# TensorE's queue in traced order, woven from four chains, with score products of four heads side by side

## The chip, the cores and the metric

The kernel runs on one core of a Trainium2 chip. The metric is the device time of one execution in microseconds; a kernel's time is the median of its runs. In the text PE is TensorE's matmuls, PEld its weight loads, DVE VectorE, ACT ScalarE, POOL GpSimd and SP the queue that issues most DMAs. `L382` is line 382 of the kernel before, unless the text says that it is of the one after.

## The reference, cut to what matters

Eight sequences of 512 tokens with 128 channels pass two layers. Everything is float32.

```python
# layer 0
h  = layernorm(x) * (1 + ca) + sa
xn = ln1(h)
attn = softmax(mask(q k^T / sqrt(8))) v        # 16 heads of 8, causal, 512 x 512
xc = silu(conv4(xn @ in_x));  dt = softplus(...);  B, C from xc @ x_proj
for t:  s = exp(dt A) s + dt xc B;  y = C s    # 256 channels, 16 states, 512 steps
y  = (y + xc D) * silu(xn @ in_z)
h  = h + alpha (attn @ o_w) + (1 - alpha) (y @ ssm_out)
h  = h + gelu(ln2(h) @ f1) @ f2;   x = x + ga * h
hm = layernorm(x) * (1 + cb) + sb
x  = x + gb * (shared(hm) + sum over the 2 best of 8 experts of gate * expert(hm))
# layer 1: attention over the 8 sequences at one position (8 heads), then
xr, xk = mixes of x and x one token earlier
x  = x + gb * sigmoid(xr Wr) * (relu(xk Wk)^2 Wv)
```

An expert is `silu(hm @ We1) @ We2` with a hidden width of 512. The kernel computes all eight and the shared one for every token, and weights them.

## The kernel before, in words

Activations lie with channels on the partitions, one sequence ("batch" b) as a tile of 128 x 512. All batches' residuals stay in `xT` (L146). A scheduler puts the instructions of each engine in an order, from the order of tracing, the buffers and its own idea of times; every engine then works through its own queue in that order. Buffers of a pool with the same tag are used in turn, and a tile waits until the readers of the one before in its buffer are done.

Layer 0, for each batch b:
- `head` (L620) loads x, does two layer norms and then `ssm_inputs` (L496): convolution, gates, B and C, and dt. B and C go to memory and are read back to all partitions. `layernorm` (L206) is a chain: mean by a matmul (L209), subtraction on DVE (L211), square on ACT (L213), variance by eight small matmuls (L217), power -0.5 on POOL (L226), spreading by matmuls (L230), product on DVE (L237), scale on ACT (L240).
- `ssm_scan` (L572) does the recurrence: in 8 steps of two states for each of two channel halves, ACT makes `da` (L585), DVE makes `hs` (L589) and scans it twice (L593), POOL multiplies by C (L596), DVE and POOL add it up (L604, L605). `so` (L611) projects the result.
- `attention` (L344) works on four groups g of four heads, each head on 32 partitions. `maxima` (L361) makes q and k (L364, L370), then per pair of heads and query block `qi` two score products of 32 rows (L382), two mask products (L390) and the negative row maximum on DVE (L393). `values` (L401) transposes the maxima (L406), adds them to q (L411), and per pair and key block `kj` makes the transposed scores (L419), masks (L427), the exponential on ACT (L431) and two value products of 32 columns (L435). `projected` (L446) divides by the sums (L452, L460, L464, L471) and projects (L474).
- `tail` (L631) does ln2, the feed-forward part (L639, L643, L648), a layer norm and `routing` (L665), a row of small DVE operations. `experts` (L733) does nine experts: four first products (L745), SiLU on ACT (L749), four accumulating second products (L756), the weighting (L764) and the sum on POOL (L767). `dispatch` (L722) sends the gates to memory; L753 reads one expert's gates to all partitions.

Scores lie in the pool `psc` (two buffers of two banks), values in `pacc` (one bank), all other products in `pmm` (three buffers of one bank, one tag).

The order of tracing is made by `together` (L197), which takes a piece of each of its parts in turn, up to a `yield`. For each batch the parts are attention b; the scan of b, and after it the head of b+1; `finish` of b-1 (tail and experts); and from b = 3 twelve pieces of layer 1's attention of a pair of batches (`attention2`, L254):

```python
            together(
                attention(b, xn, h),
                chain(ssm_scan(b, h, *scanned), head(b + 1) if b + 1 < NB else ()),
                behind or (),
                islice(second, 12) if second else (),
            )
```

Layer 1 takes the last pair's attention, adds all attentions to `xT` (L812), and then treats batch after batch from L821: layer norm, two mixes (L828, L831), three products (L836, L840, L845), a transposition (L852) and the store.

Of the kernel before, what the change touches and what calls it, by code (L numbers as in the profile page):

```python
# [33 lines left out]
EPS = 1e-5  # L34

# [36 lines left out]
def kernel(  # L72
# [20 lines left out]
    pmm = ctx.enter_context(tc.tile_pool(name="pmm", bufs=3, space=PSUM))  # L93
    psc = ctx.enter_context(tc.tile_pool(name="psc", bufs=2, space=PSUM))
    pacc = ctx.enter_context(tc.tile_pool(name="pacc", bufs=1, space=PSUM))
    dram = ctx.enter_context(tc.tile_pool(name="dram", bufs=2, space=DRAM))
    io = ctx.enter_context(tc.tile_pool(name="io", bufs=2))
    lnp = ctx.enter_context(tc.tile_pool(name="lnp", bufs=2))
# [48 lines left out]


    mods = []
    with tc.tile_pool(name="modp", bufs=1) as modp:  # L150
# [3 lines left out]
        for l in range(2):  # L154
# [6 lines left out]
            ps = pmm.tile([P, 512], F32, tag="mm", name=f"modps{l}")  # L161
# [35 lines left out]
    def together(*parts):  # L197

        parts = [iter(p) for p in parts]
        while parts:  # L200
            parts = [p for p in parts if next(p, parts) is None]

    def mm_tile(name):
        return pmm.tile([P, 512], F32, tag="mm", name=name)

    def layernorm(dst, src, scale, bias, name):  # L206

        mps = mm_tile(f"{name}_m")
        nc.tensor.matmul(mps, lhsT=mean_w, rhs=src, start=True, stop=True)  # L209
        d = lnp.tile([P, T], F32, tag="ln_d", name=f"{name}_d")  # L210
        nc.vector.tensor_sub(d, src, mps)  # L211
        sq = lnp.tile([P, T], F32, tag="ln_s", name=f"{name}_s")
        nc.scalar.activation(sq, d, AF.Square)  # L213

        vps = mm_tile(f"{name}_v")
# [8 lines left out]
        sd = lnp.tile([P, NTT], F32, tag="ln_r", name=f"{name}_r")  # L224
        nc.vector.tensor_scalar(sd, vps[:, :NTT], EPS, None, ALU.add)
        nc.gpsimd.tensor_tensor(sd, sd, mhalf, ALU.pow)  # L226

        rps = mm_tile(f"{name}_rb")
# [11 lines left out]
        nc.scalar.activation(dst, d, AF.Identity, bias=bias, scale=scale)  # L240

# [12 lines left out]
    def attention2(sp, at):  # L254

        hT = at.tile([P, NB, 2, U], F32, tag="pr", name=f"hT{sp}")
        for k in range(2):
            b = 2 * sp + k
            layernorm(hT[:, :, k, :], xT[:, b, :], mod(1, 1, b), mod(1, 0, b), f"lnc{b}")
            yield  # L260
        qkv = at.tile([P, NB, 3, C], F32, tag="qkv", name=f"qkv{sp}", bufs=1)
        for i in range(NB):
            ps = mm_tile(f"qkv{sp}_{i}")
            nc.tensor.matmul(
                ps[:, : 3 * C],
                lhsT=hT[:, i, :, :].rearrange("p s u -> p (s u)"),
                rhs=cwb("qkv"),
                start=True,
                stop=True,
            )  # L270
            nc.vector.tensor_add(
                qkv[:, i, :, :].rearrange("p k c -> p (k c)"), ps[:, : 3 * C], crow("qkv_b")
            )
            if i % 2:
                yield

        sc = at.tile([P, NB, NB, H1], F32, tag="sc", name=f"sc{sp}", bufs=1)
        for i in range(NB):
            pr = at.tile([P, NB, C], F32, tag="pr", name=f"pr{sp}_{i}")
# [9 lines left out]
            yield  # L289
# [17 lines left out]
        for i in range(NB):  # L307
            pr = at.tile([P, NB, C], F32, tag="pr", name=f"pv{sp}_{i}")
# [9 lines left out]
            yield  # L318
# [3 lines left out]
    def load_x(b):  # L322
        xin = io.tile([P, NTT, C], F32, tag="xio", name=f"xin{b}")
        nc.sync.dma_start(out=xin, in_=x[b].rearrange("(j p) c -> p j c", p=P))
        ps = mm_tile(f"xT{b}")
# [4 lines left out]
    with ExitStack() as l0:  # L330
        act = l0.enter_context(tc.tile_pool(name="act", bufs=1))
# [12 lines left out]
        def attention(b, xn, h):  # L344
# [4 lines left out]
            for j in range(NTT):  # L349
                ps = mm_tile(f"v{b}_{j}")  # L350
                nc.tensor.matmul(
                    ps[:, : NH * HV],
                    lhsT=xn[:, j * P : (j + 1) * P],
                    rhs=cw("v"),
                    start=True,
                    stop=True,
                )
                nc.vector.tensor_add(va[:, j, : NH * HV], ps[:, : NH * HV], crow("v_b"))
            qTs, kTs, sums = {}, {}, {}

            def maxima(g):  # L361

                ps = mm_tile(f"q{b}_{g}")
# [5 lines left out]
                ps = mm_tile(f"k{b}_{g}")  # L369
# [5 lines left out]
                qTs[g], kTs[g] = qT, kT  # L375
                for pr in range(2):
                    for qi in range(NTT):
                        n = (qi + 1) * P
                        ps = psc.tile([P, 2, 512], F32, tag="sc", name=f"s{b}_{g}_{pr}_{qi}")
                        for j in range(2):  # L380
                            q4 = quadrant(2 * pr + j)
                            nc.tensor.matmul(  # L382
                                ps[:, j, :n],
                                lhsT=qT[q4, qi * P : n],
                                rhs=kT[q4, :n],
                                start=True,
                                stop=False,
                            )
                        for j in range(2):
                            nc.tensor.matmul(  # L390
                                ps[:, j, qi * P : n], lhsT=ident_b, rhs=mask_b, start=False, stop=True
                            )
                        nc.vector.tensor_reduce(  # L393
                            mpads[g % 2][:, qi, 2 * pr : 2 * pr + 2, HD : HD + 1],
                            ps[:, :, :n],
                            AX.X,
                            ALU.max,
                            negate=True,
                        )

            def values(g):  # L401

                qT, kT = qTs.pop(g), kTs.pop(g)
                ps = mm_tile(f"mT{b}_{g}")
# [6 lines left out]
                nc.vector.tensor_add(qT, qT, ps)  # L411
                av = pacc.tile([P, T], F32, tag="acc", name=f"av{b}_{g}")
                for pr in range(2):
                    for kj in range(NTT):
                        n = T - kj * P
                        ps = psc.tile([P, 2, 512], F32, tag="sc", name=f"e{b}_{g}_{pr}_{kj}")
                        for j in range(2):
                            q4 = quadrant(2 * pr + j)
                            nc.tensor.matmul(  # L419
                                ps[:, j, :n],  # L420
                                lhsT=kT[q4, kj * P : (kj + 1) * P],
                                rhs=qT[q4, kj * P :],
                                start=True,
                                stop=False,
                            )
                        for j in range(2):
                            nc.tensor.matmul(  # L427
                                ps[:, j, :P], lhsT=ident_b, rhs=maskT_b, start=False, stop=True
                            )
                        ex = wk.tile([P, 2, T], F32, tag="ex", name=f"ex{b}_{g}_{pr}_{kj}")  # L430
                        nc.scalar.activation(ex[:, :, :n], ps[:, :, :n], AF.Exp)  # L431
                        for j in range(2):
                            i = 2 * pr + j
                            c0 = (4 * g + i) * HV
                            nc.tensor.matmul(  # L435
# [50 lines left out]
            for g in range(NG):  # L486
                if g + 1 < NG:
                    maxima(g + 1)
                    yield
# [502 lines left out]
```

## Time and profile before

| | us |
|---|---|
| runs | 2850.2, 2853.29, 2853.92; median 2853.29 |
| profiled execution | 2842.39 |
| its span, first to last instruction | 2840.6 |
| mean granted PE clock | 0.756 of full |
| first score maximum / last, batch 0 | 66 / 203 |
| last score maximum, batch 7 | 2385 |
| first score maxima of batches 1 to 7 | 317, 628, 926, 1263, 1566, 1905, 2208 |
| last batch: attention and scan done / first SiLU of experts / experts done | 2462 / 2525 / 2591 |
| last layer's first layer norm | 2658 |

The page shows the busy time of each engine, then the span in 40 equal slices, where a digit is the busy share in tenths. PEclk is the granted PE clock in the same slices: a matmul lasts twice as long at 5. A busy PE can be a slow one, so PE's work is best compared as busy time multiplied by the clock. A query by stretches gives, for each stretch, the busy time of PE, PEld, DVE, ACT and POOL (in brackets the number of instructions), then the clock, the DMA share and GB/s. A timeline row gives start, duration, engine, line, tiles, shapes and how many instructions were merged; in brackets, idle time before it and what ended it. An f32 product is two matmul instructions.

### The profile page before, as it was taken

The numbers are of one execution on the slowest core, as the hardware profiler recorded it, in microseconds if no ns is written. First come the engines' busy times: TensorE is split into PE (matmuls) and PEld (weight loads), VectorE is DVE, ScalarE is ACT, GpSimd is POOL, SyncE is SP. The second block draws the span as 40 slices with busy tenths as digits, with TensorE's granted clock in tenths as the row PEclk, the third lists the DMA queues.
The fourth block names the chain that finished last, engine by engine and source line by source line (L and its number), as shares of the span: only waits on it lengthen the run. The fifth ranks groups of instructions, "written<-read, shape, count | busy, mean of one in ns | idle before, by whom it ended". The sixth has DMA issues, their size and how long they took to land. (4 is left out here: it accounts for less than half of the span.)

```text
span 2840.6 us, 22315 instructions
## 1 busy us (share of the span) xinstructions
PE 2224.3 (78%) x8408; PEld 984.8 (35%) x8408; DVE 1394.0 (49%) x1734; ACT 1054.5 (37%) x1409; POOL 996.5 (35%) x587
## 2 busy tenths in 40 slices
PE   5888689878887689878987689878887689986355
PEld 3333233433343333433343333333343333433222
DVE  2861684158513864358513964358513864312522
ACT  3221434353445234353445234353435234332111
POOL 2550353036303553246203553236202553303311
PEclk9556658976898669876797769876797759888555
DMA  3100111121012101121012101121012101111000
GB/s 108 60 30 4 63 57 38 37 79 67 27 37 83 59 23 34 34 79 67 27 38 81 58 24 36 30 79 67 27 34 75 60 26 38 49 52 37 4 11 15
DMA packets 58923, 131.60 MB, mean 46 GB/s; under 512 B 6552, under 2 KB 14880, under 8 KB 58688
## 3 DMA queue, kind: packets, MB, share of 16 engines
q1 hardware_dynamic: 58336, 127.83, 14.6%
q10 hardware_dynamic: 288, 1.93, 0.2%
q8 instruction: 66, 1.08, 0.2%
q0 software_dynamic: 192, 0.42, 0.1%
q14 instruction: 41, 0.34, 0.0%
HBM read 127.41 MB, written 2.75 MB: 46 GB/s over the span
## 5 line engine op out<-in xcount | busy, mean ns | idle before, releaser
L596 POOL TENSOR_TENSOR hs<-hs,bc 128x1024 f32<-128x1024 f32 x128 | 349.1, 2728 | 260.3 <-DVE hs L593 220.7
L382 PE MATMUL s<-kT,qT 32*128 32x128 f32 (+3 forms) x1024 | 293.9, 661 | 108.9 <-DVE mpad L393 74.5
L593 DVE TENSOR_TENSOR_SCAN hs<-da,hs 128x512 f32<-128x512 f32 x256 | 376.4, 1494 | 0.0
L745 PE MATMUL e<-hm,we 128*128 128x512 f32 x576 | 338.2, 723 | 4.5 <-ACT eh L749 4.5
L749 ACT ACTIVATE eh<-e,vec_sb 128x512 f32<-128x512 f32 x288 | 191.3, 686 | 334.3 <-PE e L745 330.8
L585 ACT ACTIVATE da<-dtu,own 128x512 f32<-128x512 f32 x256 | 172.3, 714 | 379.3 <-DVE hs L593 375.1
L764 DVE SCALAR_TENSOR_TENSOR wb<-e,vec_sb,wb 128x512 f32<-128x512 f32 x64 | 47.9, 748 | 530.4 <-PE e L756 372.8
L756 PE MATMUL e<-eh,we 128*128 128x512 f32 x576 | 288.2, 631 | 23.4 <-ACT eh L749 23.4
L767 POOL TENSOR_TENSOR moe<-moe,wb 128x512 f32<-128x512 f32 x64 | 86.3, 1348 | 616.8 <-DVE wb L764 614.7
L419 PE MATMUL e<-qT,kT 32*128 32x512 f32 (+3 forms) x1024 | 256.7, 565 | 3.4 <-DVE qT L411 2.8
L435 PE MATMUL av<-ex,va 128*32 128x512 f32 (+3 forms) x1024 | 212.5, 530 | 57.0 <-ACT ex L431 56.7
L589 DVE TENSOR_TENSOR hs<-bc,dtw 128x1024 f32<-128x1024 f32 x128 | 227.4, 1778 | 50.0 <-POOL dtw L569 40.1
L605 POOL TENSOR_TENSOR xc<-xc,hs 128x512 f32<-128x512 f32 x112 | 200.7, 1792 | 138.4 <-DVE hs L604 131.8
L393 DVE TENSOR_REDUCE mpad<-s 128x2 f32<-128x256 f32 (+3 forms) x256 | 204.5, 813 | 62.9 <-PE s L390 62.3
L431 ACT ACTIVATE ex<-e 128x1024 f32<-128x1024 f32 (+3 forms) x256 | 172.2, 699 | 162.1 <-PE e L427 160.1
L745 PEld LDWEIGHTS e<-hm,we 128*128 128x128 f32 x576 | 124.6, 235 | 140.3 <-issue 109.9
L382 PEld LDWEIGHTS s<-kT,qT 32*128 32x128 f32 x1024 | 103.6, 246 | 195.6 <-DVE mpad L393 96.8
L756 PEld LDWEIGHTS e<-eh,we 128*128 128x128 f32 x576 | 110.0, 202 | 153.6 <-issue 107.7
L604 DVE TENSOR_TENSOR hs<-hs 128x512 f32<-128x512 f32 x112 | 82.4, 736 | 120.2 <-POOL hs L596 120.2
L419 PEld LDWEIGHTS e<-qT,kT 32*128 32x128 f32 x1024 | 93.6, 216 | 98.1 <-issue 56.6
L749 ACT ACT_TABLE_LOAD x96 | 123.2, 1283 | 4.9 <-PE e L745 3.1
L435 PEld LDWEIGHTS av<-ex,va 128*32 128x32 f32 x1024 | 48.9, 120 | 193.4 <-ACT ex L431 147.0
(239 smaller groups left out, 2802.3 us busy)
## 6 DMA issues: line engine op xcount, KB each, us to landing
bc<-bc SPq DMA_DIRECT2D x128, 512.0 KB, 3.7
we<-in_w_dram SPq DMA_DIRECT2D x144, 256.0 KB, 2.7
wb<-wd SPq DMA_DIRECT2D x64, 256.0 KB, 3.3
xin<-in_x_dram SPq DMA_DIRECT2D x8, 256.0 KB, 2.8
out_dram<-xout SPq DMA_DIRECT2D x8, 256.0 KB, 2.3
wa_sb<-in_wa_dram ACTq DMA_DIRECT2D x1, 1832.0 KB
wm<-in_wmod_dram SPq DMA_DIRECT2D x2, 384.0 KB, 10.9
bc<-xd_sb SPq DMA_DIRECT2D x16, 32.0 KB, 1.7
```

Of the source, the lines that this page charges most:

```text
L382: nc.tensor.matmul(ps[:, j, :n], lhsT=qT[q4, qi * P : n], rhs=kT[q4, :n], start=True, stop=False,)
L393: nc.vector.tensor_reduce(mpads[g % 2][:, qi, 2 * pr : 2 * pr + 2, HD : HD + 1], ps[:, :, :n], AX.X, ALU.max, negate=True,)
L419: nc.tensor.matmul(ps[:, j, :n], lhsT=kT[q4, kj * P : (kj + 1) * P], rhs=qT[q4, kj * P :], start=True, stop=False,)
L435: nc.tensor.matmul(av[32 * i : 32 * i + 32, kj * P :], lhsT=va[:, kj, c0 : c0 + 32], rhs=ex[:, j, :n], start=(kj == 0), stop=(kj == NTT - 1),)
L585: nc.scalar.activation(da[:, n, :], dt[c], AF.Exp, scale=A_sb[:, c, n0 + n : n0 + n + 1])
L589: nc.vector.tensor_mul(hs, bb, dtx[c].unsqueeze(1).to_broadcast([P, NN, T]))
L593: nc.vector.tensor_tensor_scan(hs[:, n, :], da[:, n, :], hs[:, n, :], 0.0, ALU.mult, ALU.add)
L596: nc.gpsimd.tensor_mul(hs, hs, cb)
L605: nc.gpsimd.tensor_add(y, y, hs[:, 0, :])
L745: nc.tensor.matmul(ps, lhsT=we1[:, m * P : (m + 1) * P], rhs=hm, start=True, stop=True)
L749: nc.scalar.activation(t, ps, AF.Silu, bias=cv("b1", e * NFF + m))
L756: nc.tensor.matmul(ps, lhsT=we2[:, m, :], rhs=hid[m], start=(m == 0), stop=(m == NFF - 1),)
```

## The change

1. **Order.** In layer 0's loop over batches, PE's queue is taken as traced (`manual_schedule`); the other engines' queues are still ordered by the scheduler. `together` gives way to `weave`: each part names its whole cost and the stretch of the batch in which it lies (0 to 1), each `yield` names the cost of a piece, and the part that is furthest behind goes next. `ssm_inputs` is a part of its own, in 0.6 to 0.85 of the batch ahead of its own; the head of b+1 and attention2 lie in 0.1 to 0.95, the scan in 0 to 0.6, attention and `finish(b-1)` in 0 to 1. The pieces are finer: a layer norm has three.
2. **Scores.** `products` makes four heads in a burst on two score tiles (four banks), then four masks. Exponentials, values and the next group's maxima alternate. The value products of four heads stand together.
3. **Experts.** Four first products are one piece, four second products another, each of cost 3.4. `dispatch` comes after the first products of expert 1.
4. **Banks.** `pmm` is split into a lane MIX with one bank (attention, scan, heads, attention2) and a lane REST with two (tail, routing, experts). Some SBUF tags have fewer buffers: the product of attention2 has one for two, layer norms have one set for each lane, input and output no longer share two; `h` has three for two.
5. **v.** Two products go into one bank, and one DVE operation adds the bias to both.
6. **Layer 1.** It has five banks of its own, and two batches are woven.

```diff
-    pmm = ctx.enter_context(tc.tile_pool(name="pmm", bufs=3, space=PSUM))
-    psc = ctx.enter_context(tc.tile_pool(name="psc", bufs=2, space=PSUM))
-    pacc = ctx.enter_context(tc.tile_pool(name="pacc", bufs=1, space=PSUM))
+    pmm = ctx.enter_context(tc.tile_pool(name="pmm", bufs=1, space=PSUM))
...
+        return pmm.tile([P, 512], F32, tag=f"mm{lane}", name=name, bufs=2 if lane == REST else 1)
...
+    def weave(*parts):
...
+        live = []
+        for k, (pieces, whole, begin, end) in enumerate(parts):
+            live.append([begin, k, iter(pieces), (end - begin) / whole])
+        while live:
+            part = min(live)
+            cost = next(part[2], None)
+            if cost is None:
+                live.remove(part)
+            else:
+                part[0] += cost * part[3]
...
+            def products(name, n, d, mask, lhs, rhs):
+
+                tiles = [
+                    psc.tile([P, 2, 512], F32, tag="sc", name=f"{name}_{pr}") for pr in range(2)
+                ]
+                for i in range(4):
+                    nc.tensor.matmul(
+                        tiles[i // 2][:, i % 2, :n],
+                        lhsT=lhs[quadrant(i)],
+                        rhs=rhs[quadrant(i)],
+                        start=True,
+                        stop=False,
+                    )
+                for i in range(4):
+                    nc.tensor.matmul(
+                        tiles[i // 2][:, i % 2, d : d + P],
+                        lhsT=ident_b,
+                        rhs=mask,
+                        start=False,
+                        stop=True,
+                    )
+                return tiles
...
+            yield from projections(0)
+            for qi in range(NTT):
+                yield from maxima(0, qi)
             for g in range(NG):
+                yield from shifts(g)
+                others = chain(
+                    projections(g + 1) if g + 1 < NG else (), projected(g - 1) if g else ()
+                )
+                for k in range(NTT):
+                    yield from exponentials(g, k)
+                    yield next(others, 0.0)
+                    if g + 1 < NG and k:
+                        yield from maxima(g + 1, k - 1)
+                    yield from values(g, k)
+                    yield next(others, 0.0)
+                yield from others
                 if g + 1 < NG:
-                    maxima(g + 1)
-                    yield
-                if g:
-                    projected(g - 1)
-                values(g)
-                yield
-            projected(NG - 1)
+                    yield from maxima(g + 1, NTT - 1)
+            yield from projected(NG - 1)
...
             for e in range(NE + 1):
-                if e == 1:
-                    wd = dispatch(b, we)
...
                     hid.append(t)
+                yield 3.4
+                if e == 1:
+                    wd = dispatch(b, we)
+                    yield 0.5
...
+        alone(head(0), after(0))
+        with tc.manual_schedule(engines={mybir.EngineType.PE}):
+            behind, second = None, None
+            for b in range(NB):
+                h, xn = ready.pop(b)
...
+                parts = [(attention(b, xn, h), 76.0, 0.0, 1.0)]
+                parts.append((ssm_scan(b, h, *inputs.pop(b)), 9.0, 0.0, 0.6))
+                if b >= 3 and b % 2:
+                    second = attention2((b - 3) // 2, a2)
+                begun = head(b + 1) if b + 1 < NB else ()
+                parts.append((chain(begun, some(second, 17) if second else ()), 18.0, 0.1, 0.95))
+                if b + 1 < NB:
+                    parts.append((after(b + 1), 7.0, 0.6, 0.85))
+                if behind:
+                    parts.append((behind, 84.0, 0.0, 1.0))
+                weave(*parts)
+                behind = finish(b, h)
+            weave((behind, 84.0, 0.0, 1.0), (second or (), 12.0, 0.0, 1.0))
...
+        for b in range(0, NB, 2):
+            weave((mixing(b), 7.0, 0.0, 1.0), (mixing(b + 1), 7.0, 0.0, 1.0))
```

## The prediction

> **What bounds the kernel now.** I read the busy times first, then the 40 slices, then the busy time of each engine stage by stage, and last the timeline of single bursts.
>
> ```profile
> span 2840.6 us, 22315 instructions
> ...
> PE 2224.3 (78%) x8408; PEld 984.8 (35%) x8408; DVE 1394.0 (49%) x1734; ACT 1054.5 (37%) x1409; POOL 996.5 (35%) x587
> ...
> PE   5888689878887689878987689878887689986355
> DVE  2861684158513864358513964358513864312522
> PEclk9556658976898669876797769876797759888555
> ```
>
> PE leads with 78%, but PEclk says that its clock is often half: 2224.3 us at a mean clock of 0.756 are 1681 us of full-clock work, 59% of the span. No engine is full on average. DVE's digits go up to 8 or 9 and down to 1, eight times: the kernel has two kinds of stage. Batches 3 and 4, cut at the first and last step of their scans:
>
> ```profile
> 899.00:1041.00 142.00, 101.12 (x336) 45.89 (x334) 110.32 (x109) 51.67 (x72) 87.18 (x42) 0.69 0.16 50
> 1041.00:1236.00 195.00, 167.18 (x707) 73.21 (x708) 74.52 (x113) 81.62 (x105) 52.09 (x35) 0.84 0.15 44
> 1236.00:1379.00 143.00, 116.21 (x358) 48.28 (x357) 114.84 (x130) 56.15 (x77) 81.68 (x40) 0.67 0.15 52
> 1379.00:1540.00 161.00, 138.12 (x634) 60.44 (x635) 35.15 (x57) 74.69 (x94) 19.34 (x20) 0.89 0.18 52
> ```
>
> The columns are PE, PEld, DVE, ACT, POOL busy us, then the clock. While a scan runs, DVE is busy 78 to 80% of the time: DVE bounds that stage. Between scans DVE is busy 22 to 38%, PE 86% at a clock of 0.84 to 0.89. That is 167.2 x 0.84 + 138.1 x 0.89 = 263 us of full-clock PE work in 356 us: PE bounds that stage, at 0.74 us of work per us. At its end (1177 to 1241) the timeline shows DVE in the serial chain of the next batch's layer norms and scan inputs, with waits of 3 to 8 us; the next scan can't start before it is through.
>
> One burst of scores, and the last layer:
>
> ```profile
> 801.93 1.13 PE L419 MATMUL e<-qT,kT 32*128 32x512 f32 x4
> 802.99 0.28 PE L427 MATMUL e<-masks_b,ident_b 128*128 128x128 bf16 x2
> 803.21 0.92 PE L419 MATMUL e<-qT,kT 32*128 32x384 f32 x4
> ...
> 812.20 1.08 PE L464 MATMUL rb<-cst_sb,rd 128*32 128x128 f32 x32 [0.35 <-DVE rd L460]
> ```
> ```profile
> 2658.68 2.08 PE L209 MATMUL lnd_m<-xT,cst_sb 128*128 128x512 f32 x2 [0.92 <-DVE xT L812]
> ...
> 2679.95 1.12 PE L852 MATMUL oT<-cst_sb,rg 128*128 128x128 f32 x4 [2.19 <-POOL rg L849]
> 2680.86 1.91 PE L209 MATMUL lnd_m<-xT,cst_sb 128*128 128x512 f32 x2
> ```
>
> Two heads' scores (4 instructions, since each f32 product is two) and two masks take 803.21 - 801.93 = 1.28 us. In the last layer a batch's chain begins only when the one before has ended: 2680.9 - 2658.7 = 22 us each.
>
> **What the Trainium skill says.** "TensorE: Matmul & The Clock Gate", Part 3 (packing small matmuls), has products in different row groups run side by side, about 4 ns apart. The trace agrees for two row groups: single records of L419 start at 801.930 and 801.936, their second passes at 802.463 and 802.470. Four row groups occur nowhere in it; four column groups do (L464: 32 instructions in 1.08 us, four at a time). "TensorEngine Tiling (Array Packing)", Key Properties, says that a change of tiling drains the engine; the trace shows some 0.1 us of it before each mask. The clock page's Part 1 gives half clock by default and full clock after a busy window of 3.4 us; here the clock records are 0.5 or 1.0 in multiples of 3.41 us. By my count over those windows, with each matmul weighted by its share of the 128x128 array, the median window ahead of a rise was filled to 1.0, of those that stayed at half 0.41, ahead of a fall 0.16. A pair of heads fills half the array, so it doesn't raise the clock; four fill it.
>
> **The change, part by part.** Durations are means of the groups of before; positions are those of the built programs' instructions on each engine.
>
> Four heads side by side. Two pairs at 512 columns are 2.56 us; four heads are 1.06 (first product to first mask, 801.93 to 802.99) + 0.35 (four masks instead of two in 0.22) = 1.41. Of the 1.15 saved, 0.86 scales with the columns (mean 320 of 512) and 0.29 doesn't: 0.83 us x 256 bursts = 211 us of full-clock work. The value products (L435) lose the same streaming and one tile change, 0.65 x 128 = 84. Together 295 of 1681. Both ends: nothing if row groups 3 and 4 queue up, 295 if they don't; I take 295. It is worth time only where PE bounds.
>
> The weave. The built order puts head(b+1) and its scan inputs inside attention b, and 8 to 10 of the 32 scans of b+1 (DVE) ahead of the end of b. The serial chain of 1177 to 1241 gets cover. But DVE's order still bunches: nearly all of a scan stands before the first maxima of the second head group. So a batch is again two stages, which I cost from the order.
> - Stage A, from the last maxima of b-1 to the first of group 1 of b. DVE's work: scan 16 x (1.78 + 2 x 1.49 + 0.74) = 88; the rest (8 maxima, three layer norms, routing, projections' readers, ends of attention) about 31 to 45, of which attention2 makes the difference. By batch 116.6, 118.8, 118.8, 133.3, 118.8, 133.3, 119.5 for b = 1 to 7: 859 us. PE has 50 to 64 us there, under cover even at half clock. At before's 80%: 1074 us.
> - Stage B, the other maxima, exponentials, values and some seven experts. PE's work per head group: exponentials 4.3, maxima 4.3, values 2.6, three experts 6 x 3.43 = 20.6, the rest 5.4: 37.2 us. B is 2.75 such groups, 102 to 111 us: 738 us for seven batches. DVE's 38 to 62 are beside it.
>
> How full is PE in B? I walked one group by hand along the queues, 0.2 us per handover. PE waits: experts' third product for the first SiLU (two banks; ACT has two exponentials and a table load of 1.28 ahead) 2.3; the one bank of the MIX lane 1.1; score tiles, since each burst takes both, 1.2 and 1.05; the shift transposes for the last two maxima (2.4 us on DVE) 2.7; small ones 0.8. Sum 9.2 on 37.2: 46.4 us, 0.80. It is the walk's figure, above the 0.74 of before, whose chain had no cover. At 0.80: 922 us.
>
> Behind a waiting PE instruction now stands everything, since the queue is in traced order: the MIX bank's reader sits on DVE or ACT behind scans or `da` (up to 3 us), and experts wait though ready. In A that costs nothing, DVE is the bound; in B it is the 20%.
>
> Experts in bursts. Same products (two passes 0.43 us apart at full clock in the timeline, 0.857 us each); a burst at half clock is 6.9 us of full array, two windows, so it raises the clock. Table loads: 242 in the built order for 225, +17 x 1.28 = 22 us on ACT, busy 37%: nothing.
>
> Small edits. `v` in two additions of 288 for four of 144: below 0.1 us saved a batch. attention2's product buffer goes from two to one: POOL 1.93 to 2.35 and DVE 1.22 to 1.93 alternate, up to 2 us x 8 in stage A of b = 4 and 6, 30 in all at most, zero at least (scans between them); it is within the 80%. Dispatch moves behind the first products of expert 1: its store and load (3.3 us to land) then end after e2's 3.4 us, up to 3 us of DVE wait in 8 batches, 24 at most, hidden at least in A's tail. SP has the same 382 transfers; the weights of expert 2 stand behind the scan's last loads, which free up before B.
>
> Ends. Batch 0 has no experts; its DVE work to its last maximum is that of before, so 203 us as before. After batch 7's last maximum: 40 us of attention (77 before, with experts between), then layer norm to first SiLU 63, experts 66, attention2 67, all as before (between 2462, 2525, 2591 and 2658, where these steps end in the trace), + 6 for eight qkv products through one bank. Last layer: two batches side by side; one chain is 22, PE is busy 11 of them, I add half of that: 27 x 4 + 4 for the last store = 112 for 182.
>
> Sum: 203 + 1074 + 922 + 40 + 63 + 66 + 73 + 112 = 2553 us of span (before 2840.6: periods -186, end of attention -37, qkv +6, last layer -70). The profiled execution took 2842.39, 1.8 over its span, and the runs' median of 2853.29 is 10.9 over that: 2566 us.
>
> **Rivals.**
> - *Better cover* (chance 0.17). A reaches 0.87 (batch 0's scan: 107.6 of 128 is 0.84), B 0.90: 987 + 820 for 1996, 2377 us. For it: ACT and POOL are at 35 to 37%. Against: every head group has the two readers' ping-pong.
> - *Four heads don't run side by side* (0.08): the 295 come back, 69% of them in B: 295 x 0.69 / 0.80 x 7/8 = 223, 2789 us. Against: L464 has four column groups.
> - *The waits pull the clock down* (0.12), and it is slower. PE's in-order stalls of 2 to 3 us in B empty a window, the clock falls to half, and B's work takes twice as long: 2 x 37.2 + 4 = 78 per group, 215 for 132, +83 x 7 = 581 if all of B. It decides from half of B at half clock (+287); at two thirds, 2953 us. For it: falls occur at a fill of 0.16, and a 2.7 us stall does that. Against: a burst of experts lifts it again.
> - *No change*: gains and stalls cancel, 0.02.
>
> **How the numbers follow.** Forecast 0.61, 2566 us, own range 2450 to 2720. Range 2400 to 2800: A at 0.75 with B at 0.68 gives 2800, A at 0.87 with B at 0.90 gives 2377, whose last 23 I leave out; the unknown costs above lie inside. Faster by over 0.2% (what a measurement can tell from no change): 0.61 + 0.17 + 0.08 = 0.86; same 0.02; slower 0.12.
>
> **What would show it.** Four records of a score burst within 20 ns; 256 bursts at about 1.06 us of streaming for 512 columns at full clock. Scans starting before the last value product of the batch ahead. Maxima of b and b+1 about 285 us apart (312 before). In stage B a clock of 0.85 or more with PE waiting for ACT's SiLU and for DVE's maxima. Last layer 27 us a pair. It is wrong if the period is over 300, if PEclk in B is below 0.75, or if DVE in A is under 75% busy.

## The result, and the profile after

| us | before | after | forecast |
|---|---|---|---|
| median of the runs | 2852.56 | 2801.64 | 2566 |
| ratio, 95% interval | | 0.982, 0.9803 to 0.9837 | |
| span of the profiled execution | 2840.6 | 2800.8 | 2553 |

It is faster by 51 us where 287 were forecast, 82 us above the forecast's own range (2450 to 2720) and 2 us above the wide one (2400 to 2800). The page of the kernel after (line numbers are its own from here on):

```profile
span 2800.8 us, 22165 instructions
...
PE 1854.6 (66%) x8408; PEld 845.0 (30%) x8408; DVE 1417.7 (51%) x1718; ACT 1066.6 (38%) x1426; POOL 1025.1 (37%) x587
...
PE   4367558855786468765588458775568547857837
...
DVE  2863782257334752277723772348832573252155
...
PEclk9557668876798669866798668886689667978958
```

PE's work fell as forecast: 1854.6 us at a clock of 0.768 are 1424 us of full-clock work, 1681 before. But the span hardly followed: PE is now idle a third of it. Batches 3 and 4, cut where the prediction cut them (A from the last maxima of a batch to the first of group 1 of the next, B from there to the last):

```profile
864.00:1033.00 169.00, 94.78 (x393) 44.98 (x397) 112.46 (x132) 71.24 (x92) 95.64 (x48) 0.65 0.18 58
1033.00:1187.00 154.00, 127.40 (x642) 55.62 (x634) 41.99 (x62) 63.35 (x84) 12.46 (x12) 0.90 0.13 39
1187.00:1366.00 179.00, 102.73 (x410) 47.94 (x411) 137.57 (x148) 67.84 (x90) 114.87 (x56) 0.68 0.17 54
1366.00:1519.00 153.00, 116.18 (x593) 49.81 (x591) 54.82 (x64) 60.48 (x82) 25.89 (x18) 0.90 0.14 39
```

DVE's work in the two A stages, 112 and 138 us, is close to what was counted (119 and 133), but the stages last 169 and 179 us: DVE is 67 and 77% busy. B has the clock that was hoped for, 0.90, but PE is busy only 83 and 76% of it. Between scores and their readers, both sides now wait for each other. From the list of waits (who waited, for whom, total us, times, longest):

```profile
DVE mpad L434 <- PE s L417: 213.3, 66, 8.6
DVE hs L665 <- POOL hs L657: 129.7, 71, 2.5
PEld e L805 <- ACT eh L809: 165.8, 141, 6.3
PE s L409 <- DVE mpad L434: 124.7, 24, 10.8
PE e L805 <- ACT eh L809: 72.1, 43, 5.4
PE lna_v L231 <- DVE kT L399: 41.1, 7, 10.1
PE ao L522 <- DVE dtu L618: 26.5, 5, 5.4
PE q L388 <- DVE va L377: 14.2, 1, 14.2
```

In the kernel before, maxima waited 62.3 us for scores, and experts' first products 4.5 us for SiLU (213.3 and 72.1 now):

```profile
DVE mpad L393 <- PE s L390: 62.3, 72, 2.8
PE e L745 <- ACT eh L749: 4.5, 9, 0.6
```

The last three lines of the list after join products and readers that have no data in common. In the line of `ao`, for one, a product of attention waits until DVE has read a product of the scan's inputs, because both use the one bank of lane MIX. The last of the three, in PE's and then in DVE's timeline:

```profile
69.59 1.33 PE L370 MATMUL v<-wa_sb,xn 128*128 128x144 f32 x4 [1.40 <-DVE va L377]
85.07 2.07 PE L388 MATMUL q<-xn,wa_sb 128*128 128x512 f32 x2 [14.15 <-DVE va L377]
```
```profile
69.09 0.44 DVE L377 TENSOR_TENSOR va<-v,row_sb 128x288 f32<-128x288 f32 x1
72.78 2.27 DVE L650 TENSOR_TENSOR hs<-bc,dtw 128x1024 f32<-128x1024 f32 x1 [3.24 <-POOL dtw L630]
76.20 1.22 DVE L650 TENSOR_TENSOR hs<-bc,dtw 128x1024 f32<-128x1024 f32 x1 [1.16 <-POOL dtw L630]
77.34 6.66 DVE L654 TENSOR_TENSOR_SCAN hs<-da,hs 128x512 f32<-128x512 f32 x4
83.93 0.72 DVE L660 SCALAR_TENSOR_TENSOR xc<-xc,vec_sb,hs 128x512 f32<-128x512 f32 x1
84.57 0.45 DVE L377 TENSOR_TENSOR va<-v,row_sb 128x288 f32<-128x288 f32 x1
```

The second `v` is ready at 70.9. Its reader stands on DVE behind the scan's first steps and comes at 84.57. Till then the bank is taken, and PE, with `q` at the head of its queue, does nothing for 14 us. And a burst of four in stage A of batch 4, with score bursts behind it (PE):

```profile
1266.30 2.71 PE L700 MATMUL f<-h,wa_sb 128*128 128x512 f32 x4
1271.10 3.68 PE L700 MATMUL f<-h,wa_sb 128*128 128x512 f32 x4 [2.09 <-ACT hid L704]
1274.71 0.50 PE L409 MATMUL s<-kT,qT 32*128 32x128 f32 x8
1275.14 0.40 PE L417 MATMUL s<-masks_b,ident_b 128*128 128x128 bf16 x4
1282.23 1.55 PE L409 MATMUL s<-kT,qT 32*128 32x256 f32 x8 [6.69 <-DVE mpad L434]
```

The lane of two banks is full after two of the four products (an `x4` row here is two f32 products). PE waits for Gelu on ACT, ahead of which ACT loads a table (1.28 us). The first score burst, whose `k` left PE at 1266.3, comes at 1274.7, when DVE has gone on with scans. Its readers are through only at 1282, and the next burst, which needs both score tiles, has waited 6.69 us for them.

### The profile page after: what moved, and what is told of

Same layout as the page of the kernel before. It is cut to its first block, busy times and chain, and to the rows that moved or that the text cites. A ratio compares the mean times of both kernels' runs of the same rounds, so it can differ in the third digit from the quotient of the medians.

```text
span 2800.8 us, 22165 instructions
## 1 busy us (share of the span) xinstructions
PE 1854.6 (66%) x8408; PEld 845.0 (30%) x8408; DVE 1417.7 (51%) x1718; ACT 1066.6 (38%) x1426; POOL 1025.1 (37%) x587
## 3 DMA queue, kind: packets, MB, share of 16 engines
HBM read 127.41 MB, written 2.75 MB: 46 GB/s over the span
## 5 line engine op out<-in xcount | busy, mean ns | idle before, releaser
L654 DVE TENSOR_TENSOR_SCAN hs<-da,hs 128x512 f32<-128x512 f32 x256 | 389.2, 1545 | 3.3 <-ACT da L646 3.1
L805 PE MATMUL e<-hm,we 128*128 128x512 f32 x576 | 325.8, 692 | 76.2 <-ACT eh L809 72.1
L434 DVE TENSOR_REDUCE mpad<-s 128x2 f32<-128x256 f32 (+3 forms) x256 | 198.5, 817 | 213.9 <-PE s L417 213.3
L409 PE MATMUL s<-kT,qT 32*128 32x128 f32 (+3 forms) x1024 | 162.0, 585 | 176.7 <-DVE mpad L434 124.7
L666 POOL TENSOR_TENSOR xc<-xc,hs 128x512 f32<-128x512 f32 x112 | 210.0, 1875 | 99.9 <-DVE hs L665 98.1
L650 DVE TENSOR_TENSOR hs<-bc,dtw 128x1024 f32<-128x1024 f32 x128 | 200.3, 1570 | 57.0 <-POOL dtw L630 45.6
L805 PEld LDWEIGHTS e<-hm,we 128*128 128x128 f32 x576 | 108.1, 213 | 261.3 <-ACT eh L809 165.8
L479 PE MATMUL av<-ex,va 128*32 128x512 f32 (+3 forms) x1024 | 125.1, 545 | 71.0 <-ACT ex L468 71.0
L665 DVE TENSOR_TENSOR hs<-hs 128x512 f32<-128x512 f32 x112 | 100.1, 894 | 129.9 <-POOL hs L657 129.7
L409 PE MATMUL e<-qT,kT 32*128 32x512 f32 (+3 forms) x1024 | 133.1, 579 | 39.1 <-DVE qT L452 25.0
L409 PEld LDWEIGHTS s<-kT,qT 32*128 32x128 f32 x1024 | 71.6, 222 | 237.5 <-DVE mpad L434 137.7
L809 ACT ACT_TABLE_LOAD x75 | 96.2, 1283 | 62.3 <-PE e L805 61.2
L417 PEld LDWEIGHTS <-ident_b 128*128 128x128 bf16 x1024 | 67.6, 108 | 148.1 <-issue 142.3
```

The source lines that it names most:

```text
L409: nc.tensor.matmul(tiles[i // 2][:, i % 2, :n], lhsT=lhs[quadrant(i)], rhs=rhs[quadrant(i)], start=True, stop=False,)
L434: nc.vector.tensor_reduce(mpads[g % 2][:, qi, 2 * pr : 2 * pr + 2, HD : HD + 1], tiles[pr][:, :, :n], AX.X, ALU.max, negate=True,)
L479: nc.tensor.matmul(avs[g][quadrant(i), kj * P :], lhsT=va[:, kj, c0 : c0 + 32], rhs=ex[i // 2][:, i % 2, :n], start=(kj == 0), stop=(kj == ...
L650: nc.vector.tensor_mul(hs, bb, dtx[c].unsqueeze(1).to_broadcast([P, NN, T]))
L654: nc.vector.tensor_tensor_scan(hs[:, n, :], da[:, n, :], hs[:, n, :], 0.0, ALU.mult, ALU.add)
L666: nc.gpsimd.tensor_add(y, y, hs[:, 0, :])
```

## The experiments

Where the kernel before was measured again beside them, its medians were 2848.8 to 2857.91 us.

**The last layer alone.** The kernel before with part 6 of the change only (the diff is cut to its loop):

```diff
-        for b in range(NB):
+        for b in range(0, NB, 2):
+            weave((mixing(b), 7.0, 0.0, 1.0), (mixing(b + 1), 7.0, 0.0, 1.0))
```

> The kernel before with the change's last layer alone (two batches woven, five banks of its own, the score and value banks given back ahead of it); layer 0 keeps before's order. Theory 1 (the change lost time in layer 0 and gained it in layer 1): layer 0 ends near 2655 as before, the last layer takes about 75 us instead of 182, so about 2740 us, ratio 0.96, which is faster than the whole change. Rival (the last layer gained only because layer 0 left its queues in another state): under 40 us gained, above 2810 us.

2741.41 us, ratio 0.961 (0.9589 to 0.9631): 108 us faster, more than the whole change. Then everything done to layer 0 costs about 60 us. The traces agree: layer 0's experts end at 2654 us, 2590 before.

**PE's order left to the scheduler.**

```diff
-        with tc.manual_schedule(engines={mybir.EngineType.PE}):
+        if True:
```

> The changed kernel, with PE's queue left to the scheduler like the others; weave, lanes, four heads and bursts stay. Theory 1 (in traced order PE stands in the serial chain at the end of each batch, some 60 us a batch, while other work would be ready): the scheduler fills part of that, 2600 to 2740 us. Rival A (the banks, one for the MIX lane and both score tiles in each burst, set the pace): they are the same here, so within 30 us of the change's 2802. Rival B (the scheduler tears the bursts apart and the clock falls): above 2850.

2492.49 us (0.8744, 0.8723 to 0.8766): 309 us below the changed kernel, with the same products, lanes and tiles, and more than either expectation had. The loss lies in the order of PE's queue, or in what that order does not forgive.

**Pairs again.** Scores and masks for two heads at a time, as before:

```diff
-                for i in range(4):
...
+                for pr in range(2):
+                    for i in range(2 * pr, 2 * pr + 2):
...
```

> The changed kernel, with each burst of scores as two pairs (two products, two masks, twice) instead of four products and four masks; order and everything else stay. Theory 1 (PE bounds only the stretch from the second group's maxima to the last group's, 22 of 32 bursts a batch): some 0.83 us x 22 x 7 = 128 us more there, up to 160 with the waits: 2900 to 2960 us. Rival (PE is nowhere the bound now, the ping-pong of score tiles is): within 40 us of 2802, as the first tile's reader starts earlier.

2877.76 us (1.0084, 1.0059 to 1.0109): four heads are worth 76 us here, between the two expectations. Two further runs put pairs into other versions:

> The scheduled version of the changed kernel (2492 us) with its score products as two pairs of heads instead of four side by side. Theory (four heads side by side saved only 76 us in the traced order because TensorE stood in other waits there; where those are gone the saving counts nearly in full): 150 to 220 us slower than 2492, 2640 to 2710 us. Rival (the stages wait for the readers of scores, VectorE and ScalarE, whatever the order): at most 76 us slower, under 2570 us.

2517.14 us: 25 us more, as the rival had it. And in the fastest version (below):

> The fastest version (2280 us) with its score products as two pairs of heads instead of four side by side. Theory (TensorE is busy 79% of that version's time, the most of all versions, so its extra 211 us of work can no longer hide in waits): 90 to 190 us slower, 2370 to 2470 us. Rival (the readers of the scores set the pace whatever the banks): at most 40 us slower, under 2320 us.

2374.23 us: 94 us more, at the low end of the theory. The saving counts only as far as PE isn't waiting for something else.

**DVE in traced order too**, with the scans' sums (L660 to L666) put off until the next step's scans are queued:

```diff
...
+                    if late:
+                        summed(*late.pop())
+                    late.append((n0, xc[c], c, hs))
...
-        with tc.manual_schedule(engines={mybir.EngineType.PE}):
+        with tc.manual_schedule(engines={mybir.EngineType.PE, mybir.EngineType.DVE}):
```

> The changed kernel, with DVE's queue in traced order as well, and in the trace each scan step's sum put behind the next step's scans, so that DVE doesn't wait for POOL's product. Theory 1 (the scheduler put a whole scan in front of the second head group on DVE, so that the period is a DVE stage plus a PE stage): the scan now lies beside the experts, DVE and PE work at the same time; periods of 319 fall to 250 to 280 us, 2330 to 2550 us in all. Rival (PE's own in-order waits set the period): no gain, 2780 us or more, since every reader on DVE now stands behind scans in the stage that PE bounds.

2686.53 us: 115 us faster, and both expectations missed. Next, the same with only DVE traced:

> TensorE's order left to the scheduler, VectorE's queue in traced order instead, with the scans' sums one step late (the version with both queues traced took 2687 us). Theory (the traced order of TensorE is what costs, whatever VectorE does): 2460 to 2540 us. Rival (in the version with both traced it was VectorE's traced order that set 2687): 2650 us or more.

2402.2 us (0.8427, 0.8403 to 0.8451): with either order of DVE, tracing PE cost some 300 us (2802 for 2492, 2687 for 2402). In the second pair DVE runs its 1718 instructions in the same order in both kernels, so that DVE's order isn't the reason there. In both, 12 of the 32 scans of each batch from 1 to 7 lie in stage A; in the changed kernel it is all 32. Without the late sums:

> The changed kernel with VectorE's queue in traced order instead of TensorE's, and the scans' sums in their place, not one step late. Theory (the late sums, which take GpSimd's product out of VectorE's way, were most of what the traced VectorE gained over 2492): 2470 to 2540 us. Rival (the traced order itself, with maxima between the scans, gained it): under 2430 us.

2770.82 us, worse than both expectations: the traced DVE is good only with late sums, which are worth 369 us there. DVE waited for POOL's product in its steps. The row of the sums in this run, and then the rows of the next step's product and of the sums in the run with late sums:

```profile
L665 DVE TENSOR_TENSOR hs<-hs 128x512 f32<-128x512 f32 x112 | 77.5, 692 | 275.3 <-POOL hs L657 275.3
```
```profile
L662 DVE TENSOR_TENSOR hs<-bc,dtw 128x1024 f32<-128x1024 f32 x128 | 174.8, 1366 | 93.6 <-POOL xc L646 89.1 <-POOL dtw L630 3.2 <-POOL xc L643 1.2
L645 DVE TENSOR_TENSOR hs<-hs 128x512 f32<-128x512 f32 x112 | 77.9, 696 | 0.0
```

The 275.3 us of idle time ahead of the sums become 0.0, but 93.6 us, nearly all for POOL, now stand ahead of the next step's product, which had 3.2 us.

**Experts over the end of a batch.** My theory then was that the woven chains all end together, so that nothing covers the chain from one attention to the next. What is left of the experts is carried into the next batch:

```diff
...
-                    parts.append((behind, 84.0, 0.0, 1.0))
...
+                parts.append((behind, 79.0, late, 1.0 + late))
```

> The changed kernel with TensorE still in traced order, but the chain of experts shifted by a fifth of a batch against attention, so that experts stand in TensorE's queue across the end of a batch, where in the changed kernel all woven chains run out together. Theory (most of the loss lies in the uncovered chain at the end of a batch): from the last maxima of a batch to the first of the next falls from 96 us to 70 to 75, 7 x 25 = 175 us less, some 15 us more after the last batch: about 2640 us. Rival (TensorE stands behind waiting instructions all over the batch, and where the experts lie makes little difference): that stretch stays above 88 us, the time above 2750 us.

2808.97 us. The theory fell: from the last maxima of a batch to the first of the next it is still 95 to 119 us for batches 2 to 7 (95 to 97 in the changed kernel).

**Bursts of two.** A `yield` after every second first product of experts and feed-forward:

```diff
...
-                yield 3.4
+                    if m % 2:
+                        yield 1.7
```

> The changed kernel, TensorE still in traced order, with the first products of experts and feed-forward woven in bursts of two instead of four, as many as their lane has banks. Theory (in a burst of four, products three and four wait for ScalarE's readers, 243 us of TensorE's waits in the changed kernel against 72 when the scheduler orders it, and all of attention queues behind them): 100 to 160 us faster than 2802, 2640 to 2700 us. Rival (TensorE then stands as long before the next late reader, since VectorE's readers of scores are behind scans anyway): above 2760 us.

2646.43 us (0.9271, 0.9251 to 0.9292): 155 us faster, as the theory had it. (The 243 us in that expectation count some time twice: the 72 us of PE's waits for SiLU lie inside PEld's 166.)

**One lane.**

```diff
-        return pmm.tile([P, 512], F32, tag=f"mm{lane}", name=name, bufs=2 if lane == REST else 1)
+        return pmm.tile([P, 512], F32, tag="mm", name=name, bufs=3)
```

> The changed kernel, TensorE still in traced order, with one lane of three banks for all, as in the kernel before, instead of one bank for attention, scan inputs and layer norms and two for the rest. Theory (with one bank each product of that lane waits for the reader of the one before it, on VectorE behind scans; about 90 us of waits of layer norms' and 57 of projections' products on readers of another chain are of this kind): 30 to 90 us faster, 2710 to 2770 us. Rival (the order of the queue decides, not the banks; in one lane the products of attention then wait for SiLU too): within 20 us of 2802, or slower.

2551.94 us (0.8941, 0.8923 to 0.8958): 250 us faster, with PE still in traced order and bursts of four. Both expectations are left far behind. The experts get a third bank by this edit too, so that it undoes more than the small lane of attention. At the start of batch 0, where `q` waited 14 us:

```profile
57.80 2.29 PE L370 MATMUL v<-wa_sb,xn 128*128 128x144 f32 x8
59.88 1.92 PE L388 MATMUL q<-xn,wa_sb 128*128 128x512 f32 x2
```

The rows of `kT`, `dtu` and `va`, 82 us together in the changed kernel, are gone from this kernel's list of waits. Stages A and B of batches 3 and 4 in that kernel:

```profile
794.00:951.00 157.00, 87.56 (x389) 43.20 (x388) 109.19 (x129) 65.99 (x88) 95.33 (x48) 0.69 0.19 61
951.00:1077.00 126.00, 116.58 (x647) 53.60 (x645) 42.58 (x62) 62.62 (x84) 12.50 (x12) 0.97 0.18 48
1077.00:1243.00 166.00, 94.94 (x408) 45.60 (x409) 129.97 (x140) 63.09 (x86) 106.14 (x53) 0.68 0.18 59
1243.00:1380.00 137.00, 113.13 (x591) 49.40 (x589) 61.87 (x72) 60.50 (x82) 31.46 (x22) 0.90 0.16 43
```

B falls from 154 and 153 to 126 and 137 us, A from 169 and 179 to 157 and 166. What waits were left on SiLU (the same columns as above):

```profile
PEld e L805 <- ACT eh L809: 57.6, 49, 2.6
PE k L395 <- ACT eh L809: 27.9, 7, 4.1
PE e L805 <- ACT eh L809: 20.5, 30, 1.8
```

**Both, and one lane under the scheduler.** First the last two edits together:

> The changed kernel, TensorE in traced order, with both undone: one lane of three banks and bursts of two. Theory (both losses are mostly the same wait, a burst that needs more banks than its lane has): 2480 to 2545 us, little below the 2552 of one lane alone. Rival (two separate waits, which add up: 2802 - 155 - 250 = 2397): under 2430 us.

2538.39 us, 14 below one lane alone, as the theory had it: most of the 155 us that bursts of two regain, one lane regains too. With three banks for all, bursts of four cost almost nothing. Then the scheduled version with one lane (the two diffs together):

> The scheduled version of the changed kernel (2492 us, two lanes) with one lane of three banks. Theory (with enough banks the traced order costs little by itself; the scheduler hid the lanes by its order, so they are worth less to it): 2440 to 2495 us, so that traced order costs 55 to 110 of the 2552 us. Rival (traced order costs as much at equal banks as before, some 300 us): under 2350 us.

2408.31 us, below the theory's 2440 but far above the rival's 2350: the lanes cost the scheduler's order 84 us, the traced order 250; and at equal banks the traced order costs 144 us by itself (2552 - 2408).

**attention2's product buffer**, two for one, in the changed kernel and in two others:

```diff
-    def attention2(sp, at, nb=1):
+    def attention2(sp, at, nb=2):
...
-                    ao = wk.tile([P, T], F32, tag="ta", name=f"ao_sb{b}", bufs=1)
+                    ao = wk.tile([P, T], F32, tag="th", name=f"ao_sb{b}", bufs=2)
```

The last two lines make room, and were not tested by themselves.

> The changed kernel with two product buffers in attention2 instead of one (the copy of the attention's output shares a buffer with the scan inputs' scratch for room). Theory (the single buffer costs what the prediction allowed, up to 2 us in each of 16 steps of four rounds, partly hidden): 15 to 30 us faster, 2772 to 2787 us. Rival (in the traced order TensorE's waits reach into that stretch and it costs more): 40 us or more; or the stretch is longer for another reason, and nothing is gained: within 6 us of 2802.

2761.65 us: 40 us, most of it in batches 4, 6 and 7 (332, 332 and 331 us from last maxima to last maxima become 319, 322 and 321).

In the scheduled version, and in the one with DVE traced and late sums:

> The scheduled version of the changed kernel (2492 us) with two product buffers in attention2 instead of one (the copy of the attention's output shares a buffer with the scan inputs' scratch for room). Theory (the single buffer makes GpSimd and VectorE take turns, up to 2 us in each of 8 steps of two halves, in the stretch between scans too): 10 to 40 us faster, 2450 to 2482 us. Rival (other work of VectorE fills those gaps): within 6 us of 2492.

2477.75 us: 15 us faster.

> The version with VectorE's queue in traced order, the scans' sums one step late and TensorE's order left to the scheduler (2402 us), with two product buffers in attention2. Theory (the gain of two buffers, 15 us in the scheduled version, is there too): 2375 to 2395 us. Rival (GpSimd's products wait for VectorE's order now, not for a buffer): within 6 us of 2402, or slower.

2383.81 us: 18 us faster.

**A version that beats both:** DVE traced with late sums, PE scheduled, two product buffers, one lane.

> The fastest version so far (2384 us: VectorE in traced order, sums one step late, two product buffers, TensorE scheduled) with one lane of three banks. Theory (readers on VectorE and ScalarE still hold the one bank of attention's lane for a few us at each projection): 15 to 60 us faster, 2325 to 2370 us. Rival (the scheduler works around the lanes): within 8 us of 2384, or slower.

2280.05 us, ratio 0.7988 (0.797 to 0.8007): 104 us from the lane, more than expected, and 20% below the kernel before. With PE traced as well, and bursts of two:

> TensorE's and VectorE's queues both in traced order, with one lane, bursts of two, sums one step late and two product buffers in attention2. Theory (with the banks, bursts and sums put right, an order written down serves as well as the scheduler's): 2340 to 2420 us. Rival (TensorE's traced order still costs 60 us or more by itself): above 2430 us.

2382.49 us, inside the theory's range by its number; but against 2280 the traced PE costs 102 us (its bursts of two, which gained 14 us with one lane above, are the other difference), which is what the rival said. With its worst waits gone, an order written down is still behind the scheduler's.

## Why the prediction was wrong

The prediction's own sum, beside the traces of the changed kernel and of three versions of it (profiled spans):

| us | forecast | after | bursts of two | one lane | both |
|---|---|---|---|---|---|
| batch 0 to its last maxima | 203 | 273 | 272 | 247 | 246 |
| stage A, seven | 1074 | 1184 | 1060 | 1111 | 1057 |
| stage B, seven | 922 | 1049 | 1004 | 913 | 951 |
| attention end, to SiLU, experts, attention2 | 242 | 221 | 234 | 207 | 217 |
| last layer | 112 | 74 | 76 | 73 | 72 |
| span | 2553 | 2801 | 2646 | 2551 | 2542 |

That one lane comes within 2 us of the forecast is luck: its A is 37 us over and batch 0 is 44 over, while the last two parts are 74 under.

**Two steps failed, with about equal weight: the walk of stage B, and "In A that costs nothing, DVE is the bound".** B took 127 us more than forecast, A 110.

In the walk it is the terms "the one bank of the MIX lane 1.1" and "experts' third product for the first SiLU (two banks ...) 2.3" us a head group. For 2.75 groups in seven batches they make 21 and 44 us, all in B. The mechanism was named, and mis-sized: the two edits that undo lanes and bursts regain 263 us together. The walk gave 0.2 us to a handover, and put a reader of the MIX bank behind scans or `da` for "up to 3 us". The traces show a bank taken for up to 14 us by a reader behind scans, and all that stands behind the waiting product on PE waits with it.

How the 263 us divide: bursts of two alone regain 155, and one lane after that 108. With bursts of two, A falls by 125 us (70 of them idle time of DVE; much of the rest is DVE's work that now lies in B) and B by 45; the prediction had put nothing in A for it. One lane after that takes 53 us out of B, 26 out of batch 0 and 17 out of the end. One lane alone takes 135 out of B and 73 out of A. So the sums are firm and the split between A and B is rough: the scheduler orders the other queues anew in each version. That the 108 are MIX's one bank, and not the third bank for the experts, was only argued, from the waits on `kT`, `dtu` and `va`. With one lane B is 9 us below the walk, but by the walk's own terms up to 65 us should have gone with the lanes; its other terms were too small by up to 56.

In A, DVE's work was counted rightly (830 us for 859). But DVE was idle for 354 us there, where the 80% left 215: by the waits in these seven stretches, 178 us for POOL (117 of them for the product of its own scan step; the kernel before had 120 of these in all), 134 for PE and 41 for ACT. So DVE was not A's only bound: PE's queue held it up as well. The longest wait of the list, maxima for scores, is not the cause in A: 171 of its 213 us lie in B. "Perfetto Trace Analysis", Optimizing Tensor Performance, says that independent products should rotate through different banks, so that the emptying of one lies beside the next product. The runs agree in kind: three banks for all products were worth 250 us with PE in traced order, 84 under the scheduler.

**Batch 0** ("as before") took 70 us more. 26 are the lanes. About 20 are not time, but a moved marker: the last maxima now stand further back in attention (31 us ahead of its last exponential, 50 before), which I counted at the end of batch 7 (77 to 40) and not here. The remaining 24 I didn't trace. In the kernel with one lane 18 of the 32 scans start before the first maxima of group 1, 4 before the change: that is the order of DVE that the prediction itself described, and didn't apply to batch 0.

**Four heads side by side** was right in mechanism: the four records of one pass start within 20 ns (419.924, 419.931, 419.938, 419.944), a 512-column burst comes 1.07 us ahead of its masks at full clock (1060.57 to 1061.64), and PE's work fell by 257 us for 295. Its worth was over-sized: 76 us, and 25 or 94 in other versions. That four heads raise the clock where pairs don't shows only in part: in batch 0, which has no experts, stage B ran at 0.72, and at 0.59 with pairs; in the fastest version it was 0.68 and 0.67.

**attention2's buffer**, 30 us at most, cost 40. I placed it in stage A; the gain of the second buffer fell in B of batches 4, 6 and 7 (33 us together). **The cover of the chain** 1177 to 1241 came in part: batch 3's scans start before the last exponential of batch 2 ends (883 and 914).

**The ends** were over-estimated. In the last layer a pair of batches takes 14.5 us in the steady state, not 27: successive pairs overlap, which "half of 11 added" left out. Layer norm to SiLU took 38 us for 63, experts 75 for 66.

**The tests it set itself.** The last maxima of batches 2 to 7 are 299 to 332 us apart (285 forecast, "wrong if over 300"), and DVE is busy 67% of A in batch 3 and 77% in batch 4 ("under 75%"); the clock in B held. By its own counts of work, A came to 0.73 and B to 0.70, where its low end was 0.75 and 0.68.

**Rivals.** "The waits pull the clock down" fell: B ran at 0.90. Yet waits in PE's order, which it named, were the loss. "Four heads don't run side by side" came within 13 us of the time (2789) by luck: they do run side by side. The sign was right because of the last layer alone: layer 0 by itself became slower.

Open is why the traced order of PE still costs 102 to 144 us at equal banks. Of the 144, 122 lie in A (1111 and 989 us with one lane), where the scheduler's version holds 24 to 31 of a batch's 32 scans for 30 to 32. That is a lead and not a cause; the two queues would have to be compared wait by wait.

## What to carry to other kernels

When a queue's order is fixed by hand, cost each small pool by how long its readers stand in their own engines' queues, not by the time from a product to a ready reader. Keep a burst within the buffers of its pool, or nearly so: against bursts of two, bursts of four cost 155 us in a lane of two banks and 14 in three shared ones. Before a pool is split so that chains don't disturb each other, ask who waits in the queue when the smaller part is full: in an in-order queue it is everyone. Work taken off a busy engine is worth only what its waits leave of it: the same edit, scores of four heads at a time for two, was worth 25, 76 or 94 us.

## What the runs showed of the hardware that was not expected

The delay of the sums, alone, also shortened operations that it doesn't touch. With DVE traced and PE scheduled, 256 scans took 371.0 us with the sums in their place and 324.3 us with late sums (mean 1489 and 1308 ns). "SBUF — State Buffer", SBUF: two separate sides, has a port pair that a VectorE operation with two SBUF inputs and a GpSimd operation that reads SBUF can't hold at once: the one that starts first keeps it to its end. The traces fit. A scan that no two-input operation of POOL overlaps takes 1205 ns at the mean in the first run (sums in their place, 172 scans) and 1210 in the second (221); those that one overlaps take 2071 (84) and 1928 (35). So late sums let fewer scans meet POOL. The timeline of the changed kernel agrees: two scans take 2.33 us at 1207.16, when POOL begins its product only at 1209.57, and 4.43 us at 1240.06, beside a product of POOL at 1240.14.
